# A relational graph layer on one core: one more product by quarters, the first edge slot on ScalarE, and the bias added by a gather

## The chip, the cores and the metric

The kernel runs on one core of a Trainium2 chip, as one launch. The metric is the device time of that launch in microseconds. A core has TensorE (matmuls, written to PSUM banks), VectorE, ScalarE and GpSimd (elementwise work; GpSimd also issues the indirect transfers), and SyncE, which issues plain transfers. Each engine runs its own instructions in order, and engines wait for one another by semaphores.

## The reference

With 1250 nodes of 1024 features, 20000 edges and 8 edge types:

```python
h = relu(layernorm(x))                       # 1250 x 1024
u = h @ root + bias
for r in range(8):                           # mean over the incoming edges of type r
    sums = segment_sum(h[src] * (type == r), dst)
    u += sums / max(count, 1) @ weight[r]
z = concat([u, h]) @ w_gate + b_gate         # w_gate: 2048 x 1024
out = x + tanh(u) * z + h * (1 - z)
```

## The kernel before

**Matrices and steps.** The kernel multiplies first and gathers afterwards: y[r] = h @ weight[r] for all nodes, and then each node sums rows of y over its edges, weighted with one over the count. Eleven matrices of 1024 x 1024 are multiplied with 1250 rows: the eight relations (0 to 7), root (8) and the two halves of w_gate (9 with h, 10 with u). This text numbers matrices from zero. The rows are ten blocks of 128; `step(s, i)` does matrix `s` for the two blocks `i` and `i + 5` together. So a matrix has five steps, steps 0 and 1 and steps 2 and 3 form *pairs*, and step 4 stands alone.

**Products by quarters.** `product` is a Strassen-Winograd scheme: seven products of half size (`A11`, `A12`, `S1` to `S4`, `A22` on the left, each with a factor of the weights on the right, S1 with T1), each of four matmuls of 128 x 512 (line 491). For a pair, some of the seven are again done by quarters, seven products of 256 columns in place of eight (line 235): class `Second` does A12 with B21, `First` A11 with B11, `Third` S4 with B22, and `Fifth` S1 with T1. `Fifth` is used where `fifths(s)` holds: matrices 1 to 4. Each of these classes has left sums of h and right sums of the weights, made by VectorE: `sums` and `next_sums` (lines 289 to 298, four operations each, 1.88 us from start to start) for `First`, `Third` and `Fifth`, all into one scratch tile called `inner`; `left`, `next_left` (226 to 231) and `right` (223) for `Second`. The left sums of `Second` depend on h alone, and are made anew for each matrix.

**What TensorE waits for.** `Fifth.early` adds two quarter products on VectorE into the first sum (line 414, called F below); `Fifth.late` needs F and the sums of `next_sums`. One of the four PSUM banks called `ps` is kept for `Fifth`'s second sum while `Fifth` is in use (`sum_bank`); it is claimed by one matmul on the identity (line 134).

**Edges.** While matrices 0 to 3 are multiplied, the edges are sorted into a table, `SLOTS` places for each node: one-hot tiles, small matmuls (1224, 1278), casts of counts (`as_bf16`, 1257, ScalarE) and scatters by GpSimd (`scatter`, 1184, 157 of them). Nodes are then put in order of their number of edges, in ten blocks. `edges(g, ...)` sums in two groups: group 0 (relations 0 to 4) during matrices 5 to 7, group 1 (relations 5 to 7) during matrices 8 and 9. `K` gives the slots of each block, 118 in group 0 and 75 in group 1. A slot is an indirect gather by GpSimd into one of five `got` tiles (1533) and a multiply-add by VectorE into the block's `u` (1538). A block's `u` starts in `first_u`: in group 0 SyncE loads the bias (1551), in group 1 GpSimd reads back the sums of group 0 (872). This is issued five slots ahead of the block's first slot, nine where rows of h @ root are added on the way. `spread` hands out the slots over the calls `between(j)` that a product makes after each part, with weights 10, 8, 13, 11 and 8 for the five steps.

**Order of work.** The order on each engine is the order of the program. SyncE stores the finished rows of y, h @ root and z (`put`, 711) and waits for each to be final, with everything behind it. GpSimd's gathers wait for a `got` tile that VectorE has freed.

## Time and profile before

| | |
|---|---|
| median of three runs | 1331.38 us (1330.55 to 1331.61) |
| the profiled execution | 1331.68 us, its span 1329.9 us |
| TensorE | busy 1315.0 us, 4212 matmul records |
| VectorE | busy 1028.2 us |
| GpSimd | busy 579.2 us |
| ScalarE | busy 279.5 us |
| VectorE's waits for gathers (1538) | 38.1 us, 28 times |

Busy times are those of one profiled execution. A line number is that of the kernel before unless the text says otherwise. An fp32 matmul of 256 or 512 columns shows as two records. In a timeline a row gives the start, the duration, the engine, the line, the operation with out<-in and the number of merged instructions; in brackets stands the idle time before it and what ended it. Starts in a pipeline are closer than durations, so the cost of one instruction in a run is the distance of starts.

### The profile page before, as it was taken

How to read it: one execution, taken by the hardware profiler on the slowest of the kernel's cores; microseconds unless marked ns; L12 is line 12 of the kernel's file. 1: busy time of each engine (PE TensorE's matmuls, PEld its weight loads, DVE VectorE, ACT ScalarE, POOL GpSimd, SP SyncE). 2: the span in 40 equal slices, each digit the busy share in tenths (PEclk: the TensorE clock that was granted, in tenths of full speed). 3: DMA queues.
4: the chain of work that ended last, by engine and by line, in shares of the span. 5: the costliest groups of instructions: out<-in, count | busy, mean ns of one | idle time of the engine just before them, and what ended most of it. 6: DMA issues, size and time to landing. Idle time of an engine off the chain costs nothing.

```text
span 1329.9 us, 13668 instructions
## 1 busy us (share of the span) xinstructions
PE 1315.0 (99%) x4212; PEld 734.2 (55%) x4212; DVE 1028.2 (77%) x2132; ACT 279.5 (21%) x547; POOL 579.2 (44%) x510
## 2 busy tenths in 40 slices
PE   9999999999999999999999999999999999999997
PEld 5444565556455546655655655565465556544443
DVE  6768977797784676558977988897788799867974
ACT  3352122122112212211221211121122112122210
POOL 0001546454655047401453546446265555715631
PEclk9999999999999999999999999999999999999999
DMA  8976355734834252144648769778788957969961
GB/s 306 302 228 165 87 96 129 155 60 77 161 103 101 81 115 49 53 159 153 221 138 305 254 236 368 261 256 275 250 280 304 353 180 246 323 249 292 326 178 60
DMA packets 116802, 263.75 MB, mean 198 GB/s; under 512 B 33150, under 2 KB 44818, under 8 KB 116592
## 3 DMA queue, kind: packets, MB, share of 16 engines
q1 hardware_dynamic: 56528, 112.62, 28.4%
q0 software_dynamic: 44064, 118.20, 28.1%
q10 hardware_dynamic: 16128, 31.98, 7.9%
q8 instruction: 33, 0.54, 0.2%
q14 instruction: 49, 0.40, 0.1%
HBM read 202.34 MB, written 75.41 MB: 209 GB/s over the span
## 4 chain that ended last, share of the span: by engine, by line
PE 81%; issue 6%; DMA 5%; DVE 5%; POOL 2%; SPq 1%; ACT 1%; POOLq 0%; DVEq 0%
PE ps_b L491 39%; PE ps L235 16%; PE ps L491 11%; PE ps_n L491 5%; PE ps_b L235 3%; PE ps_n L235 2%; DMA got<-y,idx 2%; PE ps_q L235 2%; PE ps_q L491 2%; DMA xt<-in_x_dram 1%; POOL got L1533 1%; DMA w<-in_L_gnn_weight_dram 1%; DVE u L1538 1%; POOL out_dram L878 0%; DVE h_op L472 0%
## 5 line engine op out<-in xcount | busy, mean ns | idle before, releaser
L491 PE MATMUL ps_b<-w,h_op 128*128 128x512 f32 x1464 | 659.1, 594 | 1.0 <-ACT row L595 0.8
L491 PEld LDWEIGHTS ps_b<-w,h_op 128*128 128x128 f32 x1464 | 274.4, 190 | 305.0 <-issue 294.2
L1533 POOL DMA_INDIRECT got<-y,idx x193 | 248.2, 1286 | 285.9 <-DVE u L1538 184.1
L1538 DVE SCALAR_TENSOR_TENSOR u<-got,w_of,u 128x1024 f32<-128x1024 f32 (+1 forms) x193 | 246.8, 1281 | 40.6 <-DMA got<-y,idx 38.1
L1184 POOL DMA_INDIRECT table<-row_col,at_i x157 | 172.6, 1099 | 154.6 <-DVE at_i L1180 109.0
L491 PE MATMUL ps<-w,h_op 128*128 128x512 f32 (+1 forms) x432 | 192.1, 586 | 0.8 <-ACT row L569 0.8
L491 PEld LDWEIGHTS ps<-w,h_op 128*128 128x128 f32 x432 | 81.1, 190 | 91.5 <-issue 85.9
L491 PE MATMUL ps_n<-w,h_op 128*128 128x512 f32 x208 | 94.4, 593 | 0.0
L235 PE MATMUL ps<-inner 128*128 128x256 f32 x360 | 91.6, 380 | 0.3 <-DVE inner L290 0.3
L235 PE MATMUL ps<-w,h_op 128*128 128x256 f32 x320 | 83.0, 382 | 1.0 <-ACT w L252 1.0
L235 PEld LDWEIGHTS ps<-inner 128*128 128x128 f32 x360 | 67.8, 190 | 18.6 <-issue 9.0
L517 ACT COPY row<-ps_b 128x512 f32<-128x512 f32 x53 | 31.0, 585 | 218.2 <-PE ps_b L491 218.2
L235 PEld LDWEIGHTS ps<-w,h_op 128*128 128x128 f32 x320 | 59.9, 190 | 28.8 <-issue 20.2
L595 ACT COPY row<-ps_b 128x512 f32<-128x512 f32 x54 | 31.6, 585 | 205.1 <-PE ps_b L491 205.1
L235 PE MATMUL ps<-w,w 128*128 128x256 f32 x288 | 70.8, 380 | 0.5 <-ACT w L241 0.5
L235 PEld LDWEIGHTS ps<-w,w 128*128 128x128 f32 x288 | 54.3, 190 | 20.1 <-issue 13.4
L491 PEld LDWEIGHTS ps_n<-w,h_op 128*128 128x128 f32 x208 | 39.3, 190 | 45.1 <-issue 44.2
L523 DVE TENSOR_TENSOR row<-row 128x512 f32<-128x512 f32 x44 | 30.2, 686 | 44.0 <-ACT row L517 42.5
L639 ACT COPY row<-ps_b 128x512 f32<-128x512 f32 x40 | 23.4, 585 | 175.8 <-PE ps_b L491 142.7
L1299 DVE SCALAR_TENSOR_TENSOR junk<-k_bc,key_col,before 128x128 f32<-128x128 int16 x157 | 54.8, 349 | 4.2
L552 ACT COPY row<-ps_b 128x512 f32<-128x512 f32 x54 | 31.7, 587 | 83.5 <-PE ps_b L491 76.1
L448 POOL MEMSET h_op<- 32x1024 f32 x1 | 0.9, 946 | 97.1 <-DVE rs L986 97.1
(254 smaller groups left out, 1539.9 us busy)
## 6 DMA issues: line engine op xcount, KB each, us to landing
y<-row SPq DMA_DIRECT2D x72, 512.0 KB
w<-in_L_gnn_weight_dram ACTq DMA_DIRECT2D x21, 1024.0 KB
w<-in_L_gnn_weight_dram SPq DMA_DIRECT2D x10, 1024.0 KB
w<-in_L_gnn_w_gate_dram ACTq DMA_DIRECT2D x6, 1024.0 KB
k_bc<-keys_dram SPq DMA_DIRECT2D x39, 128.0 KB
l_bc<-los_dram SPq DMA_DIRECT2D x39, 128.0 KB
h_dram<-h_op SPq DMA_DIRECT2D x9, 512.0 KB
u<-in_L_gnn_bias_dram SPq DMA_DIRECT2D x9, 512.0 KB
```

Source lines behind the costliest of these rows:

```text
L235: nc.tensor.matmul(p, a[:, k, :], b[:, k, :], start=(fresh and k == 0), stop=(k == 1), skip_group_check=True)
L448: nc.gpsimd.memset(to[n // 32 * 32:], 0.0)
L491: nc.tensor.matmul(b[:, at], aop[:, i, k, :], w.of[i][:, k, at], start=(fresh and k == 0), stop=(k == KQ - 1), skip_group_check=True)
L517: nc.scalar.copy(d, b)
L523: nc.vector.tensor_add(c22, c if lone else c22, d)
L552: nc.scalar.copy(c11, b)
L595: nc.scalar.copy(c12, b)
L639: nc.scalar.copy(c21, b)
L1184: ins = nc.gpsimd.indirect_dma_start(out=table[:, :], out_offset=bass.IndirectOffsetOnAxis(ap=at_i[:n, c:c + 1], axis=0), in_=row_col[:n, ...
L1299: nc.vector.scalar_tensor_tensor(junk, o["k_bc"][:, i, :], key_col[:, c:c + 1], before, op0=OP.is_equal, op1=OP.mult, accum_out=rank[:, c: ...
L1533: nc.gpsimd.indirect_dma_start(out=t[:n], out_offset=None, in_=y[g][:, :], in_offset=bass.IndirectOffsetOnAxis(ap=at[:n, d, k:k + 1], axis=0),
L1538: nc.vector.scalar_tensor_tensor(u[:n], t[:n], w, u[:n], op0=OP.mult, op1=OP.add)
```

## The change

1. `fifths` holds for all matrices but matrix 0: S1 T1 goes by quarters in matrices 5 to 9 too.
2. The left sums of `Second` are made in matrix 1 alone, stored to DRAM (`keep_lefts`), and loaded by SyncE for each later matrix (`load_lefts`), for the first pair at step 0, part 0, and for the second pair at step 1, part 6.
3. In group 0 a block's first slot makes `u`: its gather is issued three slots ahead, and ScalarE multiplies it with its weight into `u` one slot ahead (`scaled_slot`). The group has ten slots fewer on VectorE.
4. In group 1 SyncE loads the bias into `u`, and GpSimd's read of group 0's sums adds onto it.
5. The bank matmul on the identity is in bf16 (`touch`), with eleven small matmuls at the start in place of eight; the casts of counts go to VectorE; each scatter is followed by three one-column memsets on GpSimd; the extra part `TICK`, which a pair's first step has with `Fifth`, counts in `spread` for step 0 alone.

```diff
+    def touch(b):
+        of = ident.bitcast(BF16)[:, :P]
+        nc.tensor.matmul(b.rearrange("p (c k) -> p c k", c=CG), of,
+                         of[:, None, :].to_broadcast([P, CG, P]), start=True, stop=True)
...
+        def keep_lefts(self):
+            s, of = self.lefts()
+            nc.sync.dma_start(of, s)
+        def load_lefts(self):
+            s, of = self.lefts()
+            nc.sync.dma_start(s, of)
...
-    def fifths(s):
-        return FIFTHS[0] <= s <= FIFTHS[1]
+    def fifths(s, i=0):
+        return s > 0
...
-                if i == 0:
+                if i == 0 and s == 1:
                     waiting[0][0].left()
...
-            if two and (i, j) == (1, 6):
+            if two and (i, j) == (1, 6) and s == 1:
                 Second(fac[s], 2).left()
                 Second(fac[s], 2).next_left()
+                Second(fac[s], 2).keep_lefts()
+            if two and s > 1 and (i, j) == (0, 0):
+                waiting[0][0].load_lefts()
+            if two and s > 1 and (i, j) == (1, LEFTS_AT):
+                Second(fac[s], 2).load_lefts()
...
-            if j == (5 if s > EARLY else 4):
+            if s == 1 and j == 4:
                 e.next_left()
+                e.keep_lefts()
...
                     tc.add_to_no_dep_group("scatter", ins.ins)
+                    for _ in range(3):
+                        nc.gpsimd.memset(apart, 0.0)
...
-                        nc.scalar.copy(s_b[:, to:to + n, 0], seen[:, k:k + n])
+                        nc.vector.tensor_copy(s_b[:, to:to + n, 0], seen[:, k:k + n])
...
         def first_u(g, d):
             n = nrows(d)
             u = new_u(d)
-            if g == 0:
-                nc.sync.dma_start(u[:n], bias[None, :].to_broadcast([n, D]))
-            else:
-                rows_of(u[:n], u_dram[g - 1][:, :], node[:n, g, d:d + 1])
+            nc.sync.dma_start(u[:n], bias[None, :].to_broadcast([n, D]))
+            rows_of(u[:n], u_dram[g - 1][:, :], node[:n, g, d:d + 1], OP.add)
             return u
+        def scaled_slot(t, g, d):
+            n = nrows(d)
+            u = new_u(d)
+            nc.scalar.mul(u[:n], t[:n], w_of[:n, g, d, 0:1])
+            return u
...
-                    if t == reads[b]:
+                    if by_act:
+                        if t == starts[b] - 3:
+                            ahead[d] = slot_of(g, d, 0, idx[:, g])
+                        if t == starts[b] - 1:
+                            u[d] = scaled_slot(ahead.pop(d), g, d)
+                    elif t == reads[b]:
                         u[d] = first_u(g, d)
...
-                said[0] += (10, 8, 13, 11, 8)[at_call[0]]
+                if j != TICK or at_call[0] == 0:
+                    said[0] += (10, 8, 13, 11, 8)[at_call[0]]
```

More of the change, by code (lines that the diff above doesn't have):

```diff
@@ L84, in tile_rgcn_highway @@
     TICK = 9
+    LEFTS_AT = 6
     FIFTHS = (1, 4)
@@ L120, in tile_rgcn_highway @@
     edges_dram = dram.tile([3, P, NCH], F32, name="edges_dram")
+    lefts_dram = dram.tile([2, P, 4 * H], F32, name="lefts_dram")
     val_dram = dram.tile([G, KEYS], F32, name="val_dram")
@@ L133, in sum_bank @@
                 kept.append(bank())
-                nc.tensor.matmul(kept[0].rearrange("p (c k) -> p c k", c=CG), ident,
-                                 ident[:, None, :].to_broadcast([P, CG, P]), start=True, stop=True)
+                touch(kept[0])
             return kept[0]
@@ L214, in __init__ @@
                 f1[:, k * H:(k + 1) * H].rearrange("p (k n) -> p k n", k=2) for k in range(4)]
+            self.i, self.s_all = i, f1[:, :4 * H]
             self.p1_p6, self.p5, self.p7 = f1[:, 2 * Q:3 * Q], f1[:, 3 * Q:3 * Q + H], \
@@ L223, in right, with lefts @@
             nc.vector.tensor_sub(to, a, b)
+        def lefts(self):
+            return self.s_all, lefts_dram[self.i // 2]
+        def keep_lefts(self):
[4 more added lines that the diff above has]
+            nc.sync.dma_start(s, of)
         def left(self):
@@ L686, in step @@
         two = paired(s, i)
-        narrow[0] = fifths(s)
+        narrow[0] = fifths(s, i)
         if not narrow[0]:
@@ L697, in step @@
             waiting[i] = Second(fac[s], i), t[0]
-            if fifths(s):
+            if fifths(s, i):
                 waiting_fifth[s, i] = Fifth(fac[s], i, room, p5_room)
@@ L849, in tile_rgcn_highway @@
     make_identity(nc, ident)
-    for _ in range(IDLE - CG):
+    touch(sum_bank(0))
+    for _ in range(IDLE - 1):
         nc.tensor.matmul(bank()[:, :P], ident, ident, start=True, stop=True)
-    nc.tensor.matmul(sum_bank(0).rearrange("p (c k) -> p c k", c=CG), ident,
-                     ident[:, None, :].to_broadcast([P, CG, P]), start=True, stop=True)
     eps = const.tile([P, 1], F32, name="eps")
@@ L1528, in as_reciprocals, with slot_of @@
             nc.vector.reciprocal(rcp, rcp)
-        def add_slot(u, g, d, k, at, w):
+        def slot_of(g, d, k, at):
             n = nrows(d)
@@ L1536, in add_slot @@
                 bounds_check=y[g].shape[0] - 1, oob_is_err=False)
+            return t
+        def add_slot(u, g, d, k, at, w):
+            n = nrows(d)
+            t = slot_of(g, d, k, at)
             w = w[:n, d, k:k + 1]
@@ L1549, in first_u @@
             u = new_u(d)
-            if g == 0:
-                nc.sync.dma_start(u[:n], bias[None, :].to_broadcast([n, D]))
-            else:
-                rows_of(u[:n], u_dram[g - 1][:, :], node[:n, g, d:d + 1])
+            nc.sync.dma_start(u[:n], bias[None, :].to_broadcast([n, D]))
+            rows_of(u[:n], u_dram[g - 1][:, :], node[:n, g, d:d + 1], OP.add)
+            return u
+        def scaled_slot(t, g, d):
+            n = nrows(d)
+            u = new_u(d)
+            nc.scalar.mul(u[:n], t[:n], w_of[:n, g, d, 0:1])
             return u
@@ L1561, in edges @@
             nb = len(blocks)
-            starts = [late + sum(K[g][d] for d in blocks[:b]) for b in range(nb + 1)]
+            by_act = int(g == 0)
+            starts = [late + sum(K[g][d] - by_act for d in blocks[:b]) for b in range(nb + 1)]
             leaves = [starts[b + 1] - 1 + GOT for b in range(nb)]
@@ L1565, in edges @@
                          leaves[b - UB] if b >= UB else -1) for b, d in enumerate(blocks)]
-            u, then = {}, {}
+            u, then, ahead = {}, {}, {}
             for t in range(-1, leaves[-1] + 4):
@@ L1569, in edges @@
                     if starts[b] <= t < starts[b + 1]:
-                        k = t - starts[b]
+                        k = t - starts[b] + by_act
                         add_slot(u[d], g, d, k, idx[:, g], w_of[:, g])
@@ L1761, in tile_rgcn_highway @@
         next(first_group)
-        s, i = beside(first_group, sum(K[0]) + LATE + 1, s, i, R0[2] - 1)
+        s, i = beside(first_group, sum(K[0]) - ND + LATE + 1, s, i, R0[2] - 1)
         passes = nc.values_load(n_pass[0:1, 0:1], min_val=0, max_val=E // MORE,
```

## The prediction

> **What bounds the kernel.** I read the page first, then the engines by window, then the timelines of TensorE, VectorE, GpSimd and SyncE around single steps. The page's first part and the windows from each matrix's fifth step to the next one's (start of its first product; columns: PE, PEld, DVE, ACT and POOL busy, granted clock, DMA share, GB/s) give the frame:

> ```profile
> PE 1315.0 (99%) x4212; PEld 734.2 (55%) x4212; DVE 1028.2 (77%) x2132; ACT 279.5 (21%) x547; POOL 579.2 (44%) x510
> ```

> ```profile
> 472.90:587.10 114.20, 114.20 (x379) 70.97 (x378) 74.14 (x145) 23.22 (x48) 48.78 (x44) 1.00 0.34 84
> ...
> 702.90:818.80 115.90, 115.90 (x355) 66.39 (x354) 98.12 (x129) 20.82 (x42) 56.78 (x47) 1.00 0.80 277
> ...
> 1050.90:1166.70 115.80, 115.80 (x353) 66.38 (x352) 102.01 (x128) 20.73 (x42) 69.91 (x52) 1.00 0.80 271
> ```

> TensorE is busy throughout at full granted clock (1.00), so time is its instructions and whatever makes it wait. VectorE comes second: 74 us where no edges are added (first window row), 98 and 102 us where they are. What one matmul costs is the distance of starts, in TensorE's timeline of a pair's first step:

> ```profile
> 736.60 3.60 PE L491 MATMUL ps_b<-w,h_op 128*128 128x512 f32 x8
> 740.03 1.03 PE L235 MATMUL ps<-w,h_op 128*128 128x256 f32 x4
> 740.90 3.68 PE L491 MATMUL ps_b<-w,h_op 128*128 128x512 f32 x8
> ```

> Eight records of 512 columns take 3.43 us (0.429 each), four of 256 take 0.87 (0.216 each). A half-width matmul costs half. Four 128-row terms in fp32 are eight records.

> **S1 T1 by quarters.** The built orders show, for matrices five to nine (two pairs each): 80 matmuls of 512 columns fewer, 140 of 256 more, so 160 records of 0.429 (68.6 us) against 280 of 0.216 (60.4 us): minus 8.2 us. A second reading: the first window above is a matrix that already has the quarters, 114.2 us; the others take 115.7 to 115.9 (one 116.4, with one wait of half a microsecond). 1.6 us times five is 8.0. I take 8.2.

> [...]

> **VectorE's share of it.** Per pair the quarters add eight sums (four of 256 and four of 512 columns: 743.36 to 745.24 for a set of four, 1.88 us, twice) and two adds of 0.34: 4.4 us, 8.9 per matrix. Loading the left sums from DRAM removes eight operations of 0.34 to 0.45 per matrix, 2.9. Making the first slot's u on ScalarE removes ten slots of 1.24 in the first group, 4.1 per matrix of three. Net plus 1.9 for matrices five to seven, plus 6.0 for eight and nine. In the last window row that is 108 us of 114.2: it fits, with 6 us to spare, if VectorE is not made to wait.

> Does it fit in each step? I laid the new VectorE order over the timeline of the pair's first step (time 0 = its first quarter product, 730.46 in the second window). T3 ends at 3.0 (733.47) as now; one slot (1.24) and the sums (1.88) end at 6.2; First's add (0.34), a slot, T4 (2.2) and a slot put F at 11.1 to 11.4, and the two next sums that the late quarters need first (0.94) at 12.4. TensorE, after the quarters, S2 and S3, wants them at 14.8. Slack 2.4. In the pair's second step: late quarters want the sums at 58.9, they stand at 56.8: slack 2.1. In matrix nine one more slot lies ahead: slack 1.0. The stage without edges shows no wait from the same code. So the quarters alone cost nothing, but a late transfer of over 1 to 2 us in VectorE's queue now reaches TensorE. For that tightness I add 0.7 (from 0 to 3: the waits for gathers are 38.1 us in 28 cases now, 1.4 each).

> **Bias joins u in the second group.** Before, GpSimd reads u back alone. Now SyncE first writes the bias, and GpSimd's read adds onto it, so GpSimd waits for a transfer that stands in SyncE's queue behind the row stores; behind GpSimd's wait are the gathers, behind these VectorE's slots, behind these the sums. Before, GpSimd comes to these reads early, and SyncE to its stores late:

> ```profile
> 996.59 1.20 POOL L1533 DMA_INDIRECT got<-y,idx  x1 [1.29 <-DVE u L1538]
> 998.09 1.11 POOL L872 DMA_INDIRECT u<-u_dram,node  x1 [0.30 <-issue]
> 1002.70 0.99 POOL L1533 DMA_INDIRECT got<-y,idx  x1 [3.50 <-DVE u L1538]
> ...
> 1072.19 2.06 POOL L872 DMA_INDIRECT u<-u_dram,node  x1 [0.30 <-issue]
> 1074.89 1.26 POOL L1533 DMA_INDIRECT got<-y,idx  x1 [0.64 <-DVE u L1538]
> ```

> ```profile
> 1005.49 4.17 SPq L711 DMA_DIRECT2D hr_dram<-row  x2
> ...
> 1079.35 0.80 SPq L711 DMA_DIRECT2D hr_dram<-row  x2
> ```

> The bias transfers' line, GpSimd's first gather of the first group (which waited for a bias), and the adding reads that the kernel has already:

> ```profile
> L1551 SPq DMA_DIRECT2D u<-in_L_gnn_bias_dram x10: 382/443/1055, 616.4 to 921.5; - x10
> ```

> ```profile
> 621.08 1.02 POOL L1533 DMA_INDIRECT got<-y,idx  x1 [59.87 <-DMA u<-in_L_gnn_bias_dram]
> ```

> ```profile
> L872 POOL DMA_INDIRECT u<-hr_dram,node x3: 1821/2004/2102, 1088.7 to 1136.3; - x3
> ```

> VectorE at the same place, already late for a gather by 2 us:

> ```profile
> 1009.03 6.43 DVE L1538 SCALAR_TENSOR_TENSOR u<-got,w_of,u 128x1024 f32<-128x1024 f32 x5
> ...
> 1017.45 1.28 DVE L1538 SCALAR_TENSOR_TENSOR u<-got,w_of,u 128x1024 f32<-128x1024 f32 x1 [1.99 <-DMA got<-y,idx]
> ```

> GpSimd reaches the fourth block's read at 998.1, seven us before the stores of the pair's end (1005.5 and 1009.3), and the eighth block's at 1072.2, ahead of the stores at 1079.4. In the changed order of SyncE those blocks' biases stand right behind these stores. A bias takes 4.7 us to land (616.4 to 621.1), an adding read 2.0, a gather 6.1 (median of its landings; lowest 2.2).

> Fourth block, second pair of matrix eight (time 0 = 962.6): last store 46.7, bias issued 47.1, landed 51.8 at most (51 with less traffic), adding read over at 53.3 to 54.1 with the gap, next gather landed at 55.5 to 60.2. Two slots that depend on it (2.5) stand before F; F and two sums take 1.3: ready at 59.3 to 64.0, wanted at 58.9. TensorE waits 0.4 to 5.1. I take 4.2, nearer the median landing.

> Eighth block, first pair of matrix nine (time 0 = 1078.4): store 0.9 and 1.3, a load of left sums, bias 2.1, landed 6.8 to 8.5, read over at 9.1 to 10.8, gather at 11.3 to 16.9. One slot, F and two sums: 13.9 to 19.5, wanted at 14.8. Wait 0 to 4.7. Slot 13 of a block of 20 carries few rows, so I take a landing near the lowest: 1.5.

> The other eight reads have a store that is long done, or lie where VectorE has room: 0.

> **First slot on ScalarE, 10 times.** A scaling takes 1.05 (its row for 128x1024), with 95 us of 116 idle on that engine, and the built order sets it two slots behind its gather. If that is late (28 of 193 are, by 1.4), copies behind it wait. Bounds 0 to 2; I take 0.4.

> **The rest.** 18 transfers of 512 KB (left sums out and in, SyncE): wanted over 15 us after issue, free. 53 casts move from ScalarE to VectorE, 0.25 each there by ScalarE's rows, 13 us over three matrices where VectorE has 24 to 39 us idle each, against a gain of 2.9 per matrix from the left sums: 0, bounds -1 to +1. 471 memsets of 0.11 on GpSimd, plus a gap of 0.2 per scatter: some 80 us where it waits 109 for VectorE; no matmul waits for the table: 0. The first matmuls change kind, but TensorE idles 1.4 us there before the first block comes: 0.

> **Sum.** -8.2 + 0.7 + 4.2 + 1.5 + 0.4 = -1.4. The profiled execution took 1331.68 (span 1329.9 and 1.8 around it), 0.3 above the median of the runs, 1331.38; so 1330.0.

> **Rivals.** (a) The new waits are hidden: gathers land at their lowest, GpSimd reaches the reads later than before. Then 8.2 less 1.0: 1324.2. For it: the order gives each read five to nine slots of lead. Against: GpSimd stood seven us ahead of the stores. (b) Slower: the bias waits reach TensorE at all four reads behind a step's last store (first, fourth, seventh and eighth blocks) at up to 5.1 each, because VectorE in matrices eight and nine has only 6 us to spare per matrix and no longer catches up: 4 x 4.5 = 18, less 8.2, plus 1.1: +10.9, 1342. It decides once the waits pass 8.2 + 2.7 = 10.9, or 2.7 each. Against: at the first and seventh read the order leaves VectorE 4 us and more.

> **How the numbers follow.** 0.2% is 2.7 us, about what a measurement here can tell from no change. My case (waits of 5.5 to 11 in sum, 1328.7 to 1334.0) has 0.42; (a) and what lies towards it, waits below 5.5, has 0.40, since the lower bounds of the two reads sum to 0.4 only; (b) and what lies towards it has 0.18. So 1330.0, and the range goes from (a) to halfway towards (b): 1323.5 to 1336.

> **What would show it.** Right: matmul records 4212 + 120 from the quarters; matrices five to seven near 114.3 us; TensorE waits for "inner" or the first sum in the second pair of matrix eight (about 4 us) and the first of matrix nine; GpSimd waiting for the bias there. Wrong: no such waits (then 1324), waits also in matrices five to seven (ScalarE or VectorE is what I mis-sized), or matrices two to four changed by over 1 us each.

## The result, and the profile after

The changed kernel takes 1369.92 us (median of four runs, 1367.58 to 1371.43) against 1331.35: 38.6 us slower, ratio 1.0289 (95% interval 1.0275 to 1.0304). Its profiled execution took 1371.43 us, span 1369.6. The forecast was 1330.0 (1323.5 to 1336).

The kernel before has two times: 1330.6 to 1331.6 in two of the five groups of runs below, 1349 to 1353 in the other three, so every ratio is against the kernel before of its own group, and the group's time is named.

First the page, then TensorE's waits (engine, tile, line, what it waited for: total us, times, longest):

```profile
PE 1319.2 (96%) x4336; PEld 763.7 (56%) x4336; DVE 1041.5 (76%) x2211; ACT 294.5 (22%) x534; POOL 648.4 (47%) x981
```

```profile
PE ps L255 <- DVE inner L316: 16.1, 4, 7.5
PE ps L255 <- DVE row L283: 15.7, 4, 9.1
PE ps L255 <- DVE inner L310: 2.2, 2, 1.3
```

TensorE has 124 records more, 120 of them the quarters' (160 of 512 columns fewer, 280 of 256 more; the other four are matmuls at the start), but its busy time rose by 4.2 us where 8.2 less were counted, and its idle time went from 15 to 50 us (span less busy). Lines of the changed kernel are 20 to 44 higher than before: 235 is 255, 491 is 511, 263 is 283, 296 is 316, 1538 is 1570, 872 is 897. Where the time lies is seen by matrix. The windows' columns are those of the prediction; the granted clock is the share of its full clock that TensorE was given. They run from a mark in one matrix's fifth step to the same mark in the next, matrices five to nine; before, these five took 115.8, 115.9, 115.7, 116.4 and 115.8 us:

```profile
597.20:711.30 114.10, 114.10 (x378) 70.97 (x377) 98.15 (x166) 25.52 (x50) 48.43 (x38) 1.00 0.54 180
711.30:827.50 116.20, 114.22 (x378) 70.93 (x377) 95.06 (x132) 26.37 (x51) 56.65 (x46) 1.00 0.77 267
827.50:942.90 115.40, 114.34 (x379) 70.94 (x378) 98.92 (x136) 28.75 (x53) 62.65 (x50) 1.00 0.83 289
942.90:1084.30 141.40, 120.95 (x377) 73.48 (x376) 103.29 (x139) 23.04 (x48) 68.04 (x51) 0.93 0.85 272
1084.30:1216.80 132.50, 120.61 (x377) 74.21 (x376) 104.08 (x137) 23.22 (x48) 63.82 (x49) 0.95 0.77 250
```

Matrix five is 1.7 faster, as the quarters promise. Six and seven gave it back, six in a wait of 2.0 us and seven in one of 1.1, which the prediction had named as a sign that it is wrong. Eight and nine lose 25.0 and 16.7, and there the granted clock is 0.93 and 0.95, and TensorE is busy 121.0 and 120.6 us for work that takes 114.1 in matrix five. The fourth block's bias, followed from SyncE to TensorE:

```profile
1009.28 0.80 SPq L731 DMA_DIRECT2D hr_dram<-row  x2
1010.18 0.71 SPq L1582 DMA_DIRECT2D u<-in_L_gnn_bias_dram  x1
...
1040.04 0.32 SPq L1844 DMA_DIRECT2D last_dram<-u  x1
1040.45 0.42 SPq L1582 DMA_DIRECT2D u<-in_L_gnn_bias_dram  x1
...
1102.43 0.79 SPq L731 DMA_DIRECT2D hr_dram<-row  x2
```

```profile
1016.26 2.39 POOL L897 DMA_INDIRECT u<-u_dram,node  x1 [13.22 <-DMA u<-in_L_gnn_bias_dram]
1018.96 1.00 POOL L1560 DMA_INDIRECT got<-y,idx  x1 [0.31 <-issue]
...
1045.45 2.46 POOL L897 DMA_INDIRECT u<-u_dram,node  x1 [3.38 <-DMA u<-in_L_gnn_bias_dram]
...
1111.21 2.95 POOL L897 DMA_INDIRECT u<-u_dram,node  x1 [17.78 <-DMA u<-in_L_gnn_bias_dram]
```

```profile
1026.52 2.60 DVE L1570 SCALAR_TENSOR_TENSOR u<-got,w_of,u 128x1024 f32<-128x1024 f32 x2 [9.30 <-DMA got<-y,idx]
...
1056.48 2.61 DVE L1570 SCALAR_TENSOR_TENSOR u<-got,w_of,u 128x1024 f32<-128x1024 f32 x2 [9.99 <-DMA got<-y,idx]
```

```profile
1030.44 2.08 PE L255 MATMUL ps<-inner 128*128 128x256 f32 x4 [7.47 <-DVE inner L316]
...
1060.27 2.08 PE L255 MATMUL ps<-w,h_op 128*128 128x256 f32 x4 [9.10 <-DVE row L283]
1062.14 5.52 PE L511 MATMUL ps_b<-w,h_op 128*128 128x512 f32 x8
```

Behind the row stores (1009.28) SyncE issues the bias at 1010.18; GpSimd's read can start at 1016.26, after 13.2 us of idle time; the gather behind it is issued at 1018.96, and its slot starts on VectorE at 1026.52; the sums follow, and TensorE goes on at 1030.44. The sixth block's bias (1040.45) stands behind the store of a finished block (1040.04, line 1844), and the same chain ends at 1060.27. The last row shows the second loss: eight records that take 3.60 took 5.52. From 20 us on to the last matmul, the trace's record of the clock has four intervals at a granted clock of 0.5 ("half clock" below). They begin during the four longest waits (7.5, 9.1, 6.3 and 3.6 us) and end 4.8, 5.7, 5.6 and 5.9 us after TensorE goes on: 22 us at half speed, 11 us lost on top of the waits.

### The profile page after: what moved, and what is told of

It is laid out like the page before. It is cut to its first block, busy times and chain, and to the rows that moved or that the text cites. A ratio compares the mean times of both kernels' runs of the same rounds, so it can differ in the third digit from the quotient of the medians.

```text
span 1369.6 us, 14557 instructions
## 1 busy us (share of the span) xinstructions
PE 1319.2 (96%) x4336; PEld 763.7 (56%) x4336; DVE 1041.5 (76%) x2211; ACT 294.5 (22%) x534; POOL 648.4 (47%) x981
## 5 line engine op out<-in xcount | busy, mean ns | idle before, releaser
L1570 DVE SCALAR_TENSOR_TENSOR u<-got,w_of,u 128x1024 f32<-128x1024 f32 (+1 forms) x183 | 233.7, 1281 | 69.6 <-DMA got<-y,idx 64.1
L1209 POOL DMA_INDIRECT table<-row_col,at_i x157 | 183.9, 1171 | 119.2 <-issue 84.9
L511 PE MATMUL ps<-w,h_op 128*128 128x512 f32 (+1 forms) x352 | 156.3, 586 | 1.4 <-ACT row L589 1.1
L255 PE MATMUL ps<-inner 128*128 128x256 f32 x480 | 123.2, 386 | 18.3 <-DVE inner L316 16.1
L255 PEld LDWEIGHTS ps<-inner 128*128 128x128 f32 x480 | 91.1, 192 | 45.7 <-DVE inner L316 19.1
L255 PE MATMUL ps<-w,h_op 128*128 128x256 f32 x360 | 95.6, 389 | 16.7 <-DVE row L283 15.7
L511 PEld LDWEIGHTS ps<-w,h_op 128*128 128x128 f32 x352 | 65.7, 190 | 77.7 <-issue 70.6
L255 PEld LDWEIGHTS ps<-w,h_op 128*128 128x128 f32 x360 | 68.2, 193 | 49.4 <-issue 21.4
L1217 POOL MEMSET apart<- 128x1 f32 x471 | 54.5, 116 | 18.1
L511 PE MATMUL ps_n<-w,h_op 128*128 128x512 f32 x128 | 57.6, 593 | 0.0
L897 POOL DMA_INDIRECT u<-u_dram,node x10 | 20.7, 2067 | 57.2 <-DMA u<-in_L_gnn_bias_dram 45.3
```

The source lines that it names most:

```text
L255: nc.tensor.matmul(p, a[:, k, :], b[:, k, :], start=(fresh and k == 0), stop=(k == 1), skip_group_check=True)
L511: nc.tensor.matmul(b[:, at], aop[:, i, k, :], w.of[i][:, k, at], start=(fresh and k == 0), stop=(k == KQ - 1), skip_group_check=True)
L1209: ins = nc.gpsimd.indirect_dma_start(out=table[:, :], out_offset=bass.IndirectOffsetOnAxis(ap=at_i[:n, c:c + 1], axis=0), in_=row_col[:n, ...
L1217: nc.gpsimd.memset(apart, 0.0)
L1570: nc.vector.scalar_tensor_tensor(u[:n], t[:n], w, u[:n], op0=OP.mult, op1=OP.add)
```

## The experiments

Groups of runs: e1 to e4 (before: 1330.56), e5 to e8 (1349.07), b_again, e9, e11 and e12 (1331.6), e2b, e5b, e13 and e14 (1352.55), b_third and e14b (1349.18).

**Bias left out (e1_no_bias).**

```diff
-            nc.sync.dma_start(u[:n], bias[None, :].to_broadcast([n, D]))
-            rows_of(u[:n], u_dram[g - 1][:, :], node[:n, g, d:d + 1], OP.add)
+            rows_of(u[:n], u_dram[g - 1][:, :], node[:n, g, d:d + 1])
```

> Changed kernel, but the second group's first_u reads u back alone, as before; the bias is left out of the sum altogether. Theory (the late bias holds GpSimd, its gathers and then VectorE, and TensorE waits and then runs at half clock): the four long waits of matrices eight and nine (7.6, 9.3, 6.5 and 3.7 us) and the half clock after them go, about 27 + 11 us of the 38.6 that the change cost and the 8 us that the quarters should bring: 1324 to 1330. Rival (VectorE is simply overloaded by the quarters' sums and adds): at least half of the waits stay, 1345 or more.

1334.26 us, ratio 1.0029 (1.0019 to 1.0040). 34.6 us of the 38.6 are the bias (1.0289 less 1.0029). But the kernel stays 3.8 us above before, where the theory had it below: a second loss, of about 12 us (3.8 and the 8.2 that the quarters should bring), was not in it. TensorE's busy time and waits show that the quarters bring about what was counted (7.3 us less busy than before), and what eats it:

```profile
PE 1307.7 (98%) x4336; PEld 758.5 (57%) x4336; DVE 1041.6 (78%) x2211; ACT 294.9 (22%) x534; POOL 648.4 (49%) x981
```

```profile
PE ps L255 <- DVE row L283: 7.3, 4, 2.5
PE ps L511 <- DVE row L352: 2.8, 1, 2.8
```

In VectorE's timeline, line 283 is the second add of `to_first`, which frees a PSUM bank:

```profile
1148.48 1.28 DVE L1570 SCALAR_TENSOR_TENSOR u<-got,w_of,u 128x1024 f32<-128x1024 f32 x1 [1.75 <-DMA got<-y,idx]
1151.56 3.80 DVE L1570 SCALAR_TENSOR_TENSOR u<-got,w_of,u 128x1024 f32<-128x1024 f32 x3 [1.80 <-DMA got<-y,idx]
1155.28 0.68 DVE L282 TENSOR_TENSOR row<-row,w 128x512 f32<-128x512 f32 x1
1156.07 0.42 DVE L283 TENSOR_TENSOR row<-row,ps 128x256 f32<-128x256 f32 x1
```

The add stands behind slots, and these behind two late gathers; TensorE's next matmul starts at 1156.54, after 2.48 us of idle time. The code says why it was not there before: in a second pair `step` places `e.to_first(to)` in step 2's last part without `Fifth`, and in step 3's first part with it, behind the slots between.

```python
            elif i == 2 and q:
...
                            fourth=lambda: (e.seventh(), e.to_first(to), True))
...
            elif q:
                fill = dict(first=lambda: (root and (e.seventh(), e.to_first(to)),
```

**Edge work as before (e2_bias_in_first).** `first_u` and `edges` are those of before, the rest is the changed kernel.

> Changed kernel with the edge work of before: the first group's u begins as the bias, no first slot on ScalarE, the second group reads u back alone; quarters, loaded left sums, casts on VectorE, memsets on GpSimd stay. Full result. Theory: as e1, and a little later in matrices six and seven, where VectorE has ten slots of 1.24 us more but 24 to 39 us idle per matrix: 1323 to 1329. Rival (the first group needs the slots on ScalarE): waits appear in matrices five to seven, over 1332.

1334.71 us, ratio 1.0029 (1.0019 to 1.0039): the same as e1. That is above the theory, but not for the rival's reason, since e1 has the slots on ScalarE and is as slow. The first slot on ScalarE is worth nothing measurable, and the loss is in the quarters or in the rest.

**Bias alone (e3_bias_alone).** In the kernel before, `first_u` loads the bias in both groups and group 1 reads onto it, so the bias is counted twice.

> Kernel before, with nothing changed but that the second group's u also begins as the bias and is added onto (the bias is then counted twice). Theory (the late bias alone makes the waits; the quarters only decide how much VectorE can absorb): waits at the same four reads, each shorter by the 1 to 3 us that VectorE has more room without the quarters' sums; 20 to 40 us slower than before, 1350 to 1370, with intervals of half clock. Rival (it takes the quarters' tightness and the bias together): under 1340.

1357.29 us, ratio 1.0198 (1.0177 to 1.0220): 26.3 us slower, as the theory had it. GpSimd waited for the bias 51.5 us in seven reads, and the longest wait of TensorE was 6.2 us, against 9.1 in the changed kernel. The late bias needs no quarters.

**Bias on GpSimd's queue (e4_bias_pool).**

```diff
-            nc.sync.dma_start(u[:n], bias[None, :].to_broadcast([n, D]))
+            nc.gpsimd.dma_start(u[:n], bias[None, :].to_broadcast([n, D]))
```

> Changed kernel, with the second group's bias written by GpSimd's own queue instead of SyncE's, so it no longer stands behind the row stores and the stores of finished blocks. Full result. Theory (place in SyncE's queue makes it late): the bias is issued when GpSimd gets there, lands in 2 to 5 us and GpSimd waits that long at each of ten reads; the longest waits shrink from 9 to about 4 us: 1335 to 1352. Rival (any bias transfer ahead of the read costs the same, the queue does not matter): 1365 to 1372.

1377.81 us, ratio 1.0359 (1.0342 to 1.0376): slower still, and outside of both expectations. The bias now has no lead over the read that needs it: GpSimd waits at all ten reads.

```profile
POOL u L897 <- DMA u<-in_L_gnn_bias_dram: 60.2, 10, 10.8
```

**Which reads (e11_two_reads, e12_eight_reads).** The bias is joined at some blocks only (`d in (7, 1)`, the fourth and eighth of the group, or the other eight), and left out at the rest.

> Changed kernel with the bias joined only at the fourth and the eighth block of the second group, the two reads that the prediction priced at 4.2 and 1.5 us; the other eight blocks read u back alone, and their bias is left out. By the prediction: 5.7 us above the kernel without bias (e1_no_bias, 3.8 us above before), so 9.5 above before. Theory (each wait was priced too low and the halved clock after it left out): two waits of 6 to 8 us and 5 us for the clock, less what VectorE absorbs: 16 to 24 us above before.

> Changed kernel with the bias joined at all blocks of the second group but the fourth and the eighth, whose bias is left out: the eight reads that the prediction priced at 0. By the prediction: as e1_no_bias, 3.8 us above before. Theory (the sixth block's bias stands in SyncE's queue behind the store of a finished block, and TensorE waited 9.3 us there and 3.7 in matrix nine's last steps): waits at those two places remain, with the clock 15 to 25 us above before.

1351.48 us, ratio 1.0140 (1.0115 to 1.0166), and 1352.22 us, ratio 1.0156 (1.0140 to 1.0173). Less e1's 1.0029, the two reads cost 14.8 us where 5.7 was forecast, and the eight cost 16.9 where 0 was. The waits in each, of e11 and then of e12:

```profile
PE ps L255 <- DVE inner L316: 11.3, 2, 6.5
PE ps L255 <- DVE row L283: 7.2, 4, 2.2
```

```profile
PE ps L255 <- DVE row L283: 20.3, 4, 11.3
PE ps L255 <- DVE inner L316: 2.2, 2, 1.2
```

The fourth and eighth block's reads end in the wait for `inner`, where the forecast had them; the others in the wait for `to_first`'s bank, up to 11.3 us, and the two places where e1 shows 2.5 us each are the ones that grew (11.3 and 6.4).

**The rest alone (e9_rest_only).** e2 without the quarters in matrices five to nine: casts, memsets, loaded left sums, first matmuls.

> All parts of the change but the quarters and the bias: casts on VectorE, memsets on GpSimd, loaded left sums, the first matmuls; edges as before (bias in the first group, no ScalarE slot). Full result. Theory (these parts cost nothing, as the prediction said, and what ate the quarters' 8 us in e2 is the bank that the quarters free late): within 3 us of the kernel before. Rival (the parts taken as free cost the missing 12 us of e2): 8 to 14 us slower than before.

1328.66 us, ratio 0.9978 (0.9968 to 0.9988), 2.9 us faster than before: the theory holds, with a gain that it did not claim. Matrices five to nine take 115.8 us each; 1.7 us are gained before matrix five. So between e9 and e2 the quarters cost 6.8 us (4 to 9.5 by the ends of the two intervals) instead of bringing 8.2. The missing 15 stand in e2's trace: 7.7 us of waits for line 283, 2.2 for line 352, and three intervals of 3.4 us at half clock, 5.1. (The execution profiled took 1337.13, 2.4 above the median, so the agreement is in part luck.) Gathers that land later are not the reason: VectorE waits for them less in e2 than in e9, which has no wait of TensorE over 1.5 us. First e2, then e9:

```profile
DVE u L1570 <- DMA got<-y,idx: 28.6, 20, 3.3
```

```profile
DVE u L1570 <- DMA got<-y,idx: 37.7, 26, 3.2
```

**Quarters out, bias in (e6_no_quarters).** `fifths` as before, all else changed.

> Changed kernel without the quarters in matrices five to nine (fifths in one to four only, as before); the bias in the second group, the ScalarE slot, loaded left sums, casts and memsets stay. Theory (the bias makes the waits and quarters make them longer, by 36 us less 27): waits like those of e3_bias_alone, 1352 to 1360. Rival (the quarters bring their 8 us whatever else is there): 1375 to 1380.

1358.87 us (1358.07 to 1359.98), 11 below the changed kernel's 1369.92 of another group: within the theory's numbers. The ratio, 1.0075, is to the 1349 of its group and says little here.

**Bias early (e7_bias_early).** The load four slots ahead of where it was, the adding read three slots later.

> Changed kernel, with the second group's bias asked for four slots earlier and the adding read put three slots later in GpSimd's order (two slots ahead of the block's first). Full result. Theory (the wait is lead time between SyncE's issue and GpSimd's read, seven slots of 1.7 us or more are added): GpSimd's waits for the bias nearly vanish, 1334 to 1342, towards e1_no_bias. Rival (the adding read itself, 2 to 3 us on GpSimd, and its landing are the cost): 1355 or more.

1359.64 us (1354.75 to 1362.80). GpSimd's waits for the bias fell from 45.3 us to 4.3, as meant (first the changed kernel, then e7):

```profile
POOL u L897 <- DMA u<-in_L_gnn_bias_dram: 45.3, 6, 17.8
```

```profile
POOL u L897 <- DMA u<-in_L_gnn_bias_dram: 4.3, 1, 4.3
```

But the time fell by only 10, against the changed kernel of another group: the median lies in the rival's range, and the theory's 1334 to 1342 is far. So this way of taking GpSimd's waits for the bias away took away the smaller part of what the bias costs. What stays, in TensorE's waits:

```profile
PE ps L255 <- DVE row L283: 10.8, 4, 5.1
PE ps L511 <- DVE row L352: 6.8, 1, 6.8
```

VectorE still waits 48.8 us for gathers against 33.3 in e1. Each adding read takes 1.6 us on GpSimd against 1.0 for a plain one in e1, and moves 512 KB that e1 doesn't load (from 940 to 1060 us the DMA engines are busy for 0.90 of the time, against 0.84 in e1). The run also puts the read itself three slots later, nearer to the slots that need it. Which of these delays the gathers was not taken apart.

**The adds that free the bank (e8_after_swap, e5_to_first_ahead, e2b and e5b).** The slots of step 2's part 6 and step 3's part 0 are handed out after `to_first`, three of the seven or eight that stood ahead of it.

```diff
-            between(j)
+            if s > EARLY and root and (i, j) in ((2, 6), (3, 0)): later.append((i, j))
+            else: between(j)
...
-                fill = dict(first=lambda: (root and (e.seventh(), e.to_first(to)),
+                fill = dict(first=lambda: (root and (e.seventh(), e.to_first(to), catch_up()),
```

> Changed kernel with the same change of VectorE's order as e5_to_first_ahead, the bias as the change has it. Theory: the waits for the bank shrink by about 2 us in matrices six and seven and by up to 4 us in eight and nine, where the gathers are late; the two waits for inner (7.6 and 6.5) stay: 1358 to 1366. Rival (the late gathers alone set when TensorE goes on): 1368 to 1372.

> The kernel with the first group's bias back (e2_bias_in_first), and in VectorE's order the adds that free a PSUM bank in each second pair (to_first) set ahead of three of the seven or eight slots that stood before them, in matrices five to nine. Same work, same TensorE order. Theory (in e1 and e2 TensorE waits 1.2 to 3.4 us per matrix for that bank, because the quarters moved these adds behind the slots, which the prediction did not see): these waits go, 7 to 9 us and up to 2 us of half clock: 1323 to 1328, faster than before. Rival (VectorE is short of time as a whole): the wait only moves to the next sums, 1332 to 1337 as e2.

> As e2_bias_in_first, again, to stand on the same chip as the next three: 0.3% above before where before takes 1331; TensorE waits 7 to 10 us for to_first's adds and the third's last adds.

> As e5_to_first_ahead, again, on the same chip as e2b. Theory (the bank freed late is most of the missing time): 5 to 9 us faster than e2b, 1325 to 1329. Rival (VectorE is short of time, the wait moves to the third's last adds): within 3 us of e2b.

In the changed kernel (e8) 1373.85 us (1367.21 to 1374.85): no gain, as the rival had it. With e2's edge work, so without the late bias, 1340.6 us (e5, 1335.51 to 1343.06), then beside each other 1338.44 without the new order (e2b, 1334.19 to 1343.84) and 1339.07 with it (e5b, 1336.31 to 1339.72): the rival again. The wait for line 283 is gone and stands at the next bank, freed by the third's last adds, as e5b's waits show:

```profile
PE ps L511 <- DVE row L352: 8.1, 4, 4.8
PE ps L255 <- DVE inner L310: 1.5, 1, 1.5
```

So the order of these adds decides where TensorE waits, not how long. That the bank is the cause falls; what is left, and e14 below fits it, is that VectorE is short of time there.

**Fewer slots, fewer quarters (e13_shares, e14_quarters_to_7, e14b).**

```diff
-                    said[0] += (10, 8, 13, 11, 8)[at_call[0]]
+                    said[0] += (10, 9, 11, 10, 10)[at_call[0]]
```

```diff
     def fifths(s, i=0):
-        return s > 0
+        return 0 < s < 8
```

> e5b, and the slots spread over the five steps of a matrix as 10, 9, 11, 10, 10 instead of 10, 8, 13, 11, 8, so fewer stand in the second pair, where the waits are. Theory (place of the slots, not their number, makes the waits): 1 to 4 us faster than e5b, 1322 to 1327. Rival (VectorE is short of time as a whole): the waits move to other steps, no gain.

> e5b with the quarters left out in matrices eight and nine (the second group). By the count of matmuls 3.3 us are given back. Theory: the remaining waits for the third's last adds lie in those two matrices and were worth 2 to 7 us, so between 3 us slower and 4 us faster than e5b. If it is faster, quarters do not pay where the second group's slots are.

> As e14_quarters_to_7, on another chip: quarters in five to seven, to_first's adds ahead of three slots, bias in the first group. Theory: 4.9 us of matmuls and 2.9 of the other parts saved, 1 to 3 us of waits left: 1324 to 1328 where before takes 1331, 1328 to 1332 where before takes 1350.

1334.21 us (1331.60 to 1338.42), and 1329.90 us (1328.54 to 1331.94). Moving slots out of the second pair is worth 5 us against e5b by the medians; the ranges overlap. Leaving the quarters out of matrices eight and nine is worth 9.2, though it gives back 3.3 us of matmuls: by this difference 12.5 us of waits and half clock go. In its trace (granted clock 0.999) there is no interval of half clock between the first block and the last, and the longest wait left of these is short:

```profile
PE ps L511 <- DVE row L352: 2.0, 2, 1.7
PE ps L255 <- issue: 1.8, 1, 1.8
```

e14's ratios to before are 0.9821 (0.9776 to 0.9866) and, as e14b, 0.9876 (0.9851 to 0.9900; 1331.65 us), both in groups where before took 1349 to 1353. It beats the kernel before there, but mostly by what before itself loses in these groups (the next paragraphs): its 1329.90 and 1331.65 us stand close to the 1331.35 of before's first group. Where before takes 1331 it wasn't measured, and the changed kernel wasn't run beside it.

**The two times of before (b_again, b_third).**

> The kernel before, unchanged, for its trace on the chip that this group of runs gets: 1330 to 1332 where gathers land as in the profile of before, near 1349 (its time beside e5 to e8) where they land later. Theory: the difference between chips is TensorE waiting for VectorE behind late gathers, so the waits of its slots for gathers are over 50 us where the time is near 1349, against 38.1.

> The kernel before, unchanged, once more for its trace. Where it takes near 1350, theory: its matrices eight and nine wait for VectorE behind gathers that land later, with half clock after; where it takes 1331, the chip question stays open.

1331.96 and 1346.57 us, on one and the same chip. The expected cause is wrong: matrices five to nine take the same time in both (115.8 to 116.8 us each), and VectorE's waits for gathers are 42.9 and 33.1 us. The 14.6 us by which TensorE's work ends later are lost in matrices one to three, 6 of them from 167 us on, 1.6 at 304 and 7 from 409 us on, while the edges are sorted. TensorE's waits in b_third:

```profile
PE ps L235 <- issue: 5.5, 2, 2.9
PE ps_b L491 <- ACT row L595: 4.0, 3, 1.7
```

TensorE and ScalarE stand idle there with nothing to wait for that the profile shows (ScalarE's rows say "remote"), and two intervals of 3.4 us at half clock follow. What holds them stays open. The granted clock of the two executions is 0.998 and 0.995. The traces of e5 to e8, all from a group in which before took 1349, show no wait over 1.4 us between 100 and 600 us; these kernels have the casts on VectorE and the memsets between scatters, but that these are the reason was not tried.

## Why the prediction was wrong, step by step

- **S1 T1 by quarters, minus 8.2: right.** e1's TensorE is busy 7.3 us less than before, with one interval of 3.4 us at half clock in it. Matrix five takes 114.1 us in the changed kernel for 115.8 before: the price per record, read from the distance of starts (0.429 and 0.216 us), held.
- **VectorE tightness, 0.7 (0 to 3): the first step that failed.** It cost about 15 us (e2 against e9; 12 to 18 by the ends of the intervals). I laid F and the next sums over the timeline and found slack of 2.4, 2.1 and 1.0 us, but did not follow what else the same condition moves: `to_first` goes behind seven or eight slots, and a bank hangs on it. e5b shows that the bank is only where it surfaces. The error is in "it fits, with 6 us to spare": VectorE's room in a matrix is no room in the step where slots, gathers and sums meet.
- **Fourth block, 4.2; eighth block, 1.5: the places and the chain were right, the size was not.** The waits were 7.5 and 6.3 us. The bias landed 6.1 us after its issue (7.2 in the eighth), not 4.7; the read took 2.39 (priced 2.0), 2.95 in the eighth; the gather's slot started 7.6 us after the gather's issue, past the range's end of 6.1, and in the eighth 4.8, where the 1.5 rested on the lowest landing, 2.2. The sum priced the bias by its waits at these two reads alone, and e7 leaves most of the cost standing with nearly all of GpSimd's waits for the bias gone.
- **"The other eight reads ... 0": the second step that failed.** e12 puts them at 16.9 us. I looked for row stores ahead of a bias and left out the stores of finished blocks in the same queue, each of which waits for VectorE's last slot: VectorE late makes the store late, the store the bias, the bias the gathers, the gathers VectorE. The rows show each link of this ring; no run opened it alone, for e4, which takes the bias out of this queue, takes its lead away with it.
- **A term that was missing: the clock.** The sum priced a wait at its length. Here it was 11 us more, in the four places worked out above, and in e1 and e2, with shorter waits, 1.7 and 5.1.
- **First slot on ScalarE, 0.4: right** (e1 and e2 have the same ratio). **The rest, 0 with bounds of 1: missed on the good side**, 2.9 us.
- **The rivals.** (b) had the sign and the chain, VectorE that no longer catches up, but not all of the reads (first and seventh where the trace has the sixth and, less surely, the tenth) and no clock; its point of decision, waits of 10.9 us in sum, was passed twice over: the four longest sum to 26.4.

What stays open: why a bias with enough lead (e7) still costs some 25 us over e1 (of another group), which is most of the bias's 34.6, and the two times of before.

## What to carry to other kernels

When a condition switches a code path, list all that moves with it, the adds that free banks included, and judge an engine's slack in the step where its queues meet, not over the stage. The transfer put ahead of a gather cost more here than its lead time (of the bias's 34.6 us some 25 stayed in e7, where it had its lead): look at everything in its queue whose release depends on the engine that it will delay, because there the delay can feed itself. And don't price a wait of TensorE at its length alone: here four waits of 3.6 to 9.1 us cost 11 us more than they lasted, and one of 2.48 in e1 some 1.7.

## What the runs showed of the hardware

In e1 the length of a wait alone does not tell whether such an interval follows: one of 2.48 us had one behind it, waits of 2.50 and 2.77 us had none.

```profile
1035.93 1.13 PE L255 MATMUL ps<-w,h_op 128*128 128x256 f32 x4 [2.50 <-DVE row L283]
1036.90 3.60 PE L511 MATMUL ps_b<-w,h_op 128*128 128x512 f32 x8
...
1052.72 3.70 PE L511 MATMUL ps<-w,h_op 128*128 128x512 f32 x8 [2.77 <-DVE row L352]
```

```profile
1156.54 1.33 PE L255 MATMUL ps<-w,h_op 128*128 128x256 f32 x4 [2.48 <-DVE row L283]
1157.66 4.71 PE L511 MATMUL ps_b<-w,h_op 128*128 128x512 f32 x7
```

The changed kernel's trace was taken stretch by stretch of its grid, from 20 us on to the last matmul, and TensorE's idle time summed in each. At full clock four stretches have 2.07, 2.66, 3.41 and 3.41 us of idle time, and half clock follows each of them; all others have 1.82 or less, and it follows none. The 1.82 is from a wait of 1.98 us that the grid splits. At half clock, it goes on behind the six stretches with 0.90 us of idle time or more and ends behind the four with none.

That the grid splits e1's two longer waits too is an estimate: the starts of its last two rows, 1.12 us apart where such rows stand 0.87 apart, put the beginning of half clock near 1157.2, and steps of 3.41 counted back from there leave the 2.48 us whole and split the others into parts of about 1.6 us or less.
